# Adding the first two pairs of state products on VectorE ahead of their transposes, in a Mamba block whose order a list scheduler writes

## The chip, the cores and the metric

One NeuronCore of a Trainium2 chip runs the whole program. The metric is the device time of one execution in microseconds. The engines are named as in the profile: PE is TensorE's matmul, PEld its weight load, DVE is VectorE, ACT is ScalarE, POOL is GpSimd, and SP is the engine whose queue issues most DMAs.

## The reference

The input x has 4096 tokens of D = 1024 channels. Three residual steps follow each other, each on a layer norm of x: half an FFN with ternary weights (-1, 0, 1 times the mean absolute weight, plus a bias), a Mamba block, and the same half FFN again.

```python
x = x + 0.5 * ffn(layernorm(x))
xz = layernorm(x) @ W_in.T;  u, z = split(xz)
u = silu(conv_b + sum(conv_w[:, k] * shifted(u, k) for k in range(4)))
dt_r, B, C = split(u @ W_xproj.T)          # 64, 16 and 16 columns
dt = softplus(dt_r @ W_dt.T + b_dt)
h[n] = exp(dt * A[n]) * h_before[n] + dt * B[n] * u      # 16 states n per channel, token by token
y = sum(h[n] * C[n] for n in range(16)) + u * Dskip
x = x + (y * silu(z)) @ W_out.T
x = x + 0.5 * ffn(layernorm(x))
```

## The kernel before

The tokens are worked off in 16 chunks of T = 256 (two token tiles of 128). Inside a chunk, the Mamba block has channels on partitions and tokens along the free dimension; its 1024 channels are 8 blocks of 128, and they are worked off in two halves of 4 blocks (so a tile of a half is 128 x 4 x 256, 1024 elements in each partition).

For one half and one state n the work is this. ACT makes the decays exp(dt * A) in PSUM (line 913, two tiles of two blocks). POOL multiplies u*dt by the state's row of B (line 934) and adds what enters from the chunk before to the first token (line 941). DVE runs the recurrence over the tokens as two scans (line 966), and multiplies h by the state's row of C (line 978, in `left`): this is the product p. PE transposes p, 8 blocks of 128 x 128, into a PSUM tile y, where the transposes of all products of the half accumulate (line 998, in `summed`). So the sum over the states is taken on PE. A 17th product, n = -1, is the skip term u * Dskip, which ACT makes (line 899). When the 17 are summed, DVE multiplies y by silu(z) (line 1015, in `gate`), PE transposes the result back (line 752, in `turned`), and W_out follows (line 760), with a residual add on DVE (line 731).

Around it, per chunk: ACT and POOL make the layer norms (lines 390 to 409), PE transposes them (line 425), the FFN multiplies with x split into a high and a low part (ACT line 453, DVE line 455, PE line 497), and DVE adds its result to x (line 476). PE makes u from W_in (line 629), ACT and DVE its convolution (lines 559, 562, 574), PE the small projections for dt, B and C (lines 641, 710), and PE z from the other half of W_in (line 677), which ACT copies out and passes through silu (lines 691, 696). The rows of B and C go through DRAM and come back broadcast to all partitions (line 883).

The order of the instructions on each engine is not the order of the source. Each piece of work is a Python generator that yields requests: an engine, a duration that is written into the code, an earliest time, and a rank. `Streams.run` keeps a clock of its own, picks the request that can start first (of two with the same start, the lower rank), holds back an engine for a few hundred ns if a better rank comes soon (HOLD), and emits its instruction. It knows one resource beside the engines, `port`: requests of DVE and POOL with two operands in SBUF are not planned at the same time. Results are due at planned times kept in `ready`. Buffers are taken from and given back to pools (`Buffers`), and a request for a buffer waits until one is planned to be free. At the end the order found is fixed with dependencies, so that each engine runs its list in that order, whatever the real durations are. The pools that matter here: three PSUM banks (`banks`), three for decays, one double one for y; three tiles each for h and the products, five for the rows of B and C, five for weights. The ranks and the numbers of buffers stand at lines 52 to 61 and 208 to 226.

The z products (line 677) are issued by `rest`, which a chunk starts only when the steps behind u (`front`, from `yield DELTA` on) and both halves' dt are planned.

Of the kernel before, what the change touches and what calls it, by code (L numbers as in the profile page):

```python
# [32 lines left out]
F32 = mybir.dt.float32  # L33
F32R = mybir.dt.float32r
AF = mybir.ActivationFunctionType
ALU = mybir.AluOpType
# [16 lines left out]
REACH = 160  # L53
ISSUE, ADDED = 950, 6000
SWITCH = 1300

DECAY, ENTER, SUM, PREPARE, RECUR, GATE = 5, 1, 1, 0, 2, 2
FFN_A, NORM, U_PART, CONV, DELTA, OUT, FFN_C = 0, 0, 3, 0, 0, 2, 3

HOLD = 0, 0, 500, 100  # L60
Z = 2, 4

# [111 lines left out]
def macaron_mamba_kernel(  # L174
# [34 lines left out]
    decays = buffers(3, [P, 2, T], "da", pool_=psum)  # L209
    ys = buffers(1, [P, TT, OH], "y", pool_=psum)  # L210
    xs = buffers(6, [P, D], "x")
    xts = buffers(2, [P, NB, T], "xT")
# [3 lines left out]
    us = buffers(4, [P, HB, T], "u")  # L216
    szs = buffers(3, [P, TT, OH], "sz")
    dts = buffers(2, [P, HB, T], "dt")
# [4 lines left out]
    hs = buffers(3, [P, HB, T], "h")  # L223
    products = buffers(3, [P, HB, T], "p")
    bcs = buffers(5, [P, 2, T], "bc")
    overs = buffers(2, [P, HB, NST], "over")
# [153 lines left out]
    def stats(c, at, tiles=range(TT)):  # L380

        ln = yield from lns.take()
        sums, squares = ln[:, 0:TT], ln[:, TT : 2 * TT]
        some = slice(tiles[0], tiles[-1] + 1)
        rstd, shift, less = ln[:, 28:30][:, some], ln[:, 32:34][:, some], ln[:, 36:38][:, some]
        xn = {}
        for t in tiles:
            xn[t] = yield from tmps.take()
            end = yield act(D + 210, at[t])
            nc.scalar.activation(xn[t], x_tiles[c, t], AF.Identity, accum_out=sums[:, t : t + 1])  # L390
            end = yield pool(140, end + REACH)
            nc.gpsimd.tensor_scalar(ln[:, 36 + t : 37 + t], sums[:, t : t + 1], -1.0 / D, None, ALU.mult)
            end = yield act(D + 210, end + REACH)
            nc.scalar.activation(  # L394
                xn[t],
                x_tiles[c, t],
                AF.Square,
                bias=ln[:, 36 + t : 37 + t],
                accum_out=squares[:, t : t + 1],
            )  # L400
        end = yield pool(1050, end + REACH)
        nc.gpsimd.tensor_scalar(rstd, squares[:, some], 1.0 / D, EPS_LN, ALU.mult, ALU.add)
        nc.gpsimd.tensor_tensor(rstd, rstd, mhalf[:, some], ALU.pow)
        nc.gpsimd.tensor_tensor(shift, less, rstd, ALU.mult)
        return ln, xn, end + REACH

    def normed(c, ln, xn, t, at):
        end = yield act(D + 210, at)
        nc.scalar.activation(  # L409
            xn[t],  # L410
            x_tiles[c, t],
            AF.Identity,
            scale=ln[:, 28 + t : 29 + t],
            bias=ln[:, 32 + t : 33 + t],
        )
        return xn[t], end + REACH

# [21 lines left out]
    def ffn(c, which, rank, at, tiles=range(TT)):  # L439
# [3 lines left out]
        def split(t):  # L443
# [6 lines left out]
            def cut(g, pt, at_):  # L450
# [7 lines left out]
                if len(ends) == NB // 4:  # L458
                    ready["parts", key, t] = end + REACH
                    parts[t] = lo, hi  # L460
# [11 lines left out]
        def residual(t, cols, pf, at_):  # L472
            at_ = max(at_, (yield from when("bias", key, t)))
            end = yield dve(650, at_)
            xt = x_tiles[c, t][:, cols]
            nc.vector.scalar_tensor_tensor(xt, pf, hscl, xt, ALU.mult, ALU.add)  # L476
            if (*key, t) != ("a", 0, 1):
                banks.put(pf, end)
            ready["ffn", key, t, cols.start] = end
            if key == ("c", NC - 1):  # L480
                yield from give_out(c, t, cols, end)
# [33 lines left out]
    def as_weights_come(key, parts, residual, rank):  # L515

        for t in range(TT):
            yield from when("parts", key, t)
        y = yield from ys.take()
        groups = {(1, h): y[:, h, :] for h in range(2)}  # L520
        for h in range(2):
            groups[0, h] = yield from banks.take()
        for k in range(NB):
            yield from when("wf", k)
# [12 lines left out]
        for t in range(TT):  # L537
            los.put(parts[t][0], end)
            his.put(parts[t][1], end)
        for h in range(2):  # L540
            end = yield from when("ffn", key, 1, h * OH)
        ys.put(y, end)

# [40 lines left out]
    def front():  # L584
        for c in range(NC):
# [32 lines left out]
            for pair in range(NB // 2):  # L618
# [4 lines left out]
                for j in range(2):  # L623
# [9 lines left out]
                    weights.put(w, end)  # L633
            yield DELTA
            px = yield from banks.take()
            for half in range(2):
                at = yield from when("u", c, half)
                end = yield pe(2 * HB * T * FULL)
                for b in range(HB):
                    k = half * HB + b  # L640
                    nc.tensor.matmul(
                        px[:NXD, :T], wx[:, k, :], u[c, half][:, b, :], start=(k == 0), stop=(k == NB - 1)
                    )
            xd[c] = yield from xds.take()
            end = yield act(T, end + REACH)
            nc.scalar.copy(xd[c][RANK:NXD, 1, :], px[RANK:NXD, :T])
            for j in range(2):
                end = yield act(T)
                nc.scalar.copy(xd[c][j * RANK : (j + 1) * RANK, 0, :], px[:RANK, :T])
            banks.put(px, end)  # L650
            bc_dram[c] = dram.tile([NST, 2, T], F32, tag="bc", name=f"bcd_{c}")
            for j in range(2):
                part_ = slice(RANK + j * NST, RANK + (j + 1) * NST)
                nc.sync.dma_start(bc_dram[c][:, j, :], xd[c][part_, 1, :])
            ready["bc", c] = end + 2500
            yield from delta(c, 0, end + REACH)
            order.spawn(rest(c, xT), DELTA)

    def rest(c, xT):
        yield from delta(c, 1, 0)  # L660
        xds.put(xd[c], order.now + 2000)
        queue = streamed(z_weights, NB, 3, Z[0])
        for half in range(2):
# [72 lines left out]
    def turned(c, half, yT):  # L736
# [8 lines left out]

        yield from when("gate", c, half)
        for t in range(TT):
            pt = yield from banks.take()
            end = yield pe(HB * P * TURN)
# [24 lines left out]
    def back():  # L774
        for c in range(NC - 1):
            yield OUT
            queue = streamed(lambda i, w: out_weights(i // 2, i % 2, w), NB, 3, OUT)
            yT = []
# [20 lines left out]
            for t in range(TT):  # L799
                yield from give_out(c, t, slice(0, D), ends[t])  # L800
                xs.put(x_tiles.pop((c, t)), order.now + 6000)
        yield from last(NC - 1)
# [74 lines left out]
    def fetch():  # L877
        for c, half, n in items:
# [8 lines left out]
            coming[c, half, n] = bc  # L887
            ready["come", c, half, n] = order.now + 4000

# [13 lines left out]
    def decaying():  # L903
        for c, half, n in items:
# [3 lines left out]
            for j in range(2):  # L908
# [10 lines left out]
                decay[c, half, n, j] = da  # L919
                ready["decay", c, half, n, j] = end + REACH  # L920
            if n + 1 == NST:
# [3 lines left out]
    def enter():  # L925
        for c, half, n in items:
# [15 lines left out]
            entering[c, half, n] = h  # L942
            ready["enter", c, half, n] = end + REACH
            if n + 1 == NST:
# [9 lines left out]
    def recur():  # L954
        behind = None
        for c, half, n in items:
# [4 lines left out]
            for j in range(2):  # L961
# [6 lines left out]
                if behind and j == 0:  # L968
                    yield from left(*behind)
            order.spawn(leave(c, half, n, h, end + REACH), ENTER)  # L970
            behind = c, half, n, h
        yield from left(*behind)

    def left(c, half, n, h):
# [5 lines left out]
        product[c, half, n] = p  # L980
        ready["product", c, half, n] = end + REACH
        order.spawn(give(c, half, n, h, end), ENTER)

    def give(c, half, n, h, at):
# [3 lines left out]
    def summed():  # L988
        for c, half, n in items:
            yield from when("product", c, half, n)  # L990
            if n < 0:
                y = yield from ys.take()
            p = product.pop((c, half, n))
            end = yield pe(D * TURN)

            for t in range(TT):
                for b in range(HB):
                    nc.tensor.matmul(  # L998
                        y[:, t, b * P : (b + 1) * P],
                        p[:, b, t * P : (t + 1) * P],  # L1000
                        ident,
                        start=(n < 0 and b == 0),
                        stop=(n == NST - 1 and b == HB - 1),
                        is_transpose=True,
                        skip_group_check=True,
                    )
            products.put(p, end)
            if n + 1 == NST:
                order.spawn(gate(c, half, y, end + REACH), GATE)

    def gate(c, half, y, at):
        yield from when("z", c, half)
        z = sz[c, half]
        end = yield dve(1170, at)
        nc.vector.tensor_tensor(flat(z), flat(y), flat(z), ALU.mult)
        ys.put(y, end + REACH)
        ready["gate", c, half] = end + REACH

# [80 lines left out]
```

## Time and profile before

| what | us |
|---|---|
| median of 3 runs | 2726.5 (2725.86 to 2727.03) |
| profiled execution, whole | 2725.84 |
| its span, first to last instruction | 2724.1 |
| mean granted TensorE clock | 0.983 |
| transposes of products on PE, line 998, x4352 | 572.5 busy |
| z products on PE, line 677, x2048 records | 474.7 busy |
| scans on DVE, line 966, x1024 | 1207.7 busy, 1206 ns each |
| decays on ACT, line 913, x2048 | 938.6 busy |
| h of POOL, line 934, x512 | 1223.2 busy, 421.7 idle before them |
| table loads on ACT, 181 in all | 1283 ns each |

A row of the profile gives the line, the engine, the operation, what it writes and reads, how often; then its busy time and the mean ns of one, and behind the second bar how long the engine stood idle just before it, and for whom. Busy time of several rows of PE may overlap, since the next matmul starts before the last has drained. A matmul in f32 leaves two records.

### The profile page before, as it was taken

Reading aid. Unit: us, or ns where it says so; the run is one execution under the profiler, and the core shown is the slowest. Engines: PE = TensorE matmul, PEld = TensorE weight load, DVE = VectorE, ACT = ScalarE, POOL = GpSimd, SP = SyncE. Lnnn points to the kernel's source line nnn. Section 1 sums busy time; section 2 is a strip of 40 time slices with the busy share of each in tenths; the row PEclk is TensorE's granted clock in tenths of the full one; section 3 lists DMA queues with packets and bytes.
Section 4 is the critical chain, followed back from the end, with each engine's and each line's share of the span. In section 5 each row is a group of like instructions: output and inputs, shape, how many; then the busy total and the mean of one; then the engine's idle time right before and its main releaser. Section 6 shows DMA issues by size and latency. Waiting matters only on the chain. (4 is left out here: it accounts for less than half of the span.)

```text
span 2724.1 us, 41050 instructions
## 1 busy us (share of the span) xinstructions
PE 2568.1 (94%) x14082; PEld 2199.6 (81%) x14082; DVE 2288.3 (84%) x2404; ACT 2001.4 (73%) x4202; POOL 1815.6 (67%) x1657
## 2 busy tenths in 40 slices
PE   5797989999999999999999999999999999999988
PEld 4686878888788787888878788887888878788866
DVE  4498898978899798888879799898889879788883
ACT  3678677787877778777787877778787777877662
POOL 0367767766677585767757577686767857577761
PEclk9897999999999999999999999999999999999999
DMA  4443536455454545546554454655545554554533
GB/s 158 146 130 103 168 106 216 132 166 149 134 173 140 179 151 153 155 129 184 166 162 144 140 167 132 182 162 155 153 140 167 159 172 146 150 157 133 182 85 109
DMA packets 218553, 410.82 MB, mean 151 GB/s; under 512 B 19172, under 2 KB 85860, under 8 KB 218344
## 3 DMA queue, kind: packets, MB, share of 16 engines
q1 hardware_dynamic: 209128, 374.65, 43.3%
q0 software_dynamic: 9216, 33.56, 6.8%
q8 instruction: 110, 1.80, 0.3%
q14 instruction: 99, 0.81, 0.1%
HBM read 390.82 MB, written 17.31 MB: 150 GB/s over the span
## 5 line engine op out<-in xcount | busy, mean ns | idle before, releaser
L934 POOL TENSOR_TENSOR h<-u,bc 128x1024 f32<-128x1024 f32 x512 | 1223.2, 2389 | 421.7 <-ACT da L913 171.1
L966 DVE TENSOR_TENSOR_SCAN h<-da,h 128x512 f32<-128x512 f32 x1024 | 1207.7, 1206 | 125.6 <-ACT da L913 99.7
L913 ACT ACTIVATE da<-dt,pr 128x255 f32<-128x255 f32 x2048 | 938.6, 473 | 61.9 <-DVE h L966 32.9
L978 DVE TENSOR_TENSOR p<-h,bc 128x1024 f32<-128x1024 f32 x512 | 658.7, 1286 | 6.6 <-PE y L998 6.4
L998 PE MATMUL y<-ident,p 128*128 128x128 f32 x4352 | 572.5, 278 | 79.5 <-DVE p L978 61.1
L998 PEld LDWEIGHTS y<-ident,p 128*128 128x128 f32 x4352 | 503.9, 143 | 151.5 <-DVE p L978 95.4
L629 PE MATMUL bank<-xT,weight 128*128 128x256 f32 x2048 | 474.7, 382 | 11.4 <-ACT u L562 8.6
L677 PE MATMUL bank<-weight,xT 128*128 128x256 f32 x2048 | 474.7, 380 | 9.2 <-DMA weight<-in_w_in 9.2
L760 PE MATMUL bank<-weight,u 128*128 128x256 f32 x2016 | 467.3, 381 | 2.2 <-DMA weight<-in_w_out 1.9
L629 PEld LDWEIGHTS bank<-xT,weight 128*128 128x128 f32 x2048 | 378.6, 190 | 69.9 <-ACT u L562 21.3
L677 PEld LDWEIGHTS bank<-weight,xT 128*128 128x128 f32 x2048 | 380.2, 191 | 56.7 <-ACT da L913 9.9
L760 PEld LDWEIGHTS bank<-weight,u 128*128 128x128 f32 x2016 | 370.9, 191 | 47.2 <-DMA weight<-in_w_out 2.1
L949 ACT COPY state<-h 128x4 f32<-128x4 f32 x512 | 99.2, 194 | 292.5 <-DVE h L966 287.5
L941 POOL TENSOR_TENSOR h<-h,over 128x4 f32<-128x4 f32 x512 | 262.5, 513 | 25.2
L497 PE MATMUL bank<-wf,lo 128*128 128x512 f32 x976 | 252.3, 400 | 3.7 <-DVE lo L455 2.4
L574 DVE SCALAR_TENSOR_TENSOR u<-up,pr,u 128x256 f32<-128x256 f32 x384 | 206.4, 570 | 55.2 <-ACT u L562 42.6
L497 PE MATMUL bank<-wf,hi 128*128 128x512 f32 x976 | 245.8, 394 | 0.0
L497 PEld LDWEIGHTS bank<-wf,lo 128*128 128x128 f32 x976 | 177.7, 188 | 48.4 <-issue 4.0
L497 PEld LDWEIGHTS bank<-wf,hi 128*128 128x128 f32 x976 | 181.7, 188 | 43.0 <-issue 4.3
L865 POOL TENSOR_TENSOR over<-pr,dt 128x64 f32<-128x64 f32 x32 | 24.9, 778 | 211.3 <-ACT dt L722 211.3
L476 DVE SCALAR_TENSOR_TENSOR x<-bank,hscl,x 128x512 f32<-128x512 f32 x124 | 91.2, 737 | 71.9 <-PE bank L497 71.8
L425 PE MATMUL bank<-ident,tmp 128*128 128x128 f32 x756 | 115.9, 285 | 27.1 <-ACT tmp L409 23.4
(98 smaller groups left out, 2125.0 us busy)
## 6 DMA issues: line engine op xcount, KB each, us to landing
bc<-bcd SPq DMA_DIRECT2D x512, 256.0 KB, 3.7
weight<-in_w_out SPq DMA_DIRECT2D x128, 512.0 KB, 5.1
weight<-in_w_in SPq DMA_DIRECT2D x128, 512.0 KB, 3.7
weight<-in_w_in SPq DMA_DIRECT2D x256, 256.0 KB, 4.2
x<-hbias POOLq DMA_DIRECT2D x64, 512.0 KB, 7.9
x<-in_x SPq DMA_DIRECT2D x32, 512.0 KB, 7.3
out<-x SPq DMA_DIRECT2D x30, 512.0 KB, 4.9
weight<-in_w_ffn SPq DMA_DIRECT2D x5, 512.0 KB, 7.4
```

The costliest lines, as they stand in the source:

```text
L425: nc.tensor.matmul(pt[:, j * P : (j + 1) * P], xn[:, k * P : (k + 1) * P], ident, start=(j == 0), stop=(j == 3), is_transpose=True, skip_g ...
L497: nc.tensor.matmul(pf, x[:, k, :], wf[:, k, cols], start=(x is lo and k == 0), stop=(x is hi and k == NB - 1),)
L574: nc.vector.scalar_tensor_tensor(ub, up[:, k : k + T], tap, ub, ALU.mult, ALU.add)
L629: nc.tensor.matmul(pp[:, j, :], wt[:, k, :], xT[:, k, :], start=(k == 0), stop=(k == NB - 1))
L677: nc.tensor.matmul(pp[:, t, :], xT[:, k, t * P : (t + 1) * P], wt[:, :, i, :], start=(k == 0 and t == 0), stop=(k == NB - 1), skip_group_c ...
L760: nc.tensor.matmul(po[:, t, :], yT[:, b, t * P : (t + 1) * P], wt[:, b, :], start=(half == 0 and t == 0 and b == 0), stop=(half == 1 and b ...
L913: nc.scalar.activation(da[:, i, 1:], dt[c, half][:, b, 1:], AF.Exp, scale=a_neg[:, half * HB + b, n : n + 1],)
L934: nc.gpsimd.tensor_tensor(h, u[c, half], bc[:, 0:1, :].to_broadcast([P, HB, T]), ALU.mult)
L941: nc.gpsimd.tensor_tensor(h[:, :, 0], h[:, :, 0], over[c, half][:, :, n], ALU.add)
L966: nc.vector.tensor_tensor_scan(rows_, flat(da), rows_, 0.0, ALU.mult, ALU.add)
L978: nc.vector.tensor_tensor(p, h, bc[:, 1:2, :].to_broadcast([P, HB, T]), ALU.mult)
L998: nc.tensor.matmul(y[:, t, b * P : (b + 1) * P], p[:, b, t * P : (t + 1) * P], ident, start=(n < 0 and b == 0), stop=(n == NST - 1 and b = ...
```

## The change

Six things change together.

1. A new constant PAIRED = range(0, 4, 2) names states 0 and 2. Behind the product of such a state, the new `paired` adds the product of the state before it (the skip term before 0, state 1 before 2) on DVE, in one flat 128 x 1024 addition in place, after the next state's second scan. `summed` passes over the states -1 and 1. The product pool grows from 3 to 4 tiles.
2. y is two PSUM tiles, one for each token tile, instead of one double one. `gate` runs for each token tile, 512 columns at a time, and `turned` waits for each token tile's gate.
3. The z products leave `rest` and become a stream of their own (`gates`), started right behind u with rank Z[0] = 1, and so do the steps to dt (`steps`), whose two halves of the first projection no longer stand together.
4. Planned times: products, decays, entering states and normed tiles are taken to be ready 300 ns later than before (the four LATE constants); a bias load is taken to need 9000 instead of 6000, a row of B and C 3000 instead of 4000; x tiles are taken to be free at once after their store is issued.
5. Ranks, HOLD and the prefetch of the output weights (2 instead of 3) change.
6. Buffers: x 7 instead of 6, rows of B and C 6 instead of 5, silu(z) 2 instead of 3. The two normed tiles of a layer norm are taken together.

```diff
-ISSUE, ADDED = 950, 6000
+ISSUE, ADDED = 950, 9000
...
-DECAY, ENTER, SUM, PREPARE, RECUR, GATE = 5, 1, 1, 0, 2, 2
-FFN_A, NORM, U_PART, CONV, DELTA, OUT, FFN_C = 0, 0, 3, 0, 0, 2, 3
-HOLD = 0, 0, 500, 100
-Z = 2, 4
+LATE_P, LATE_D, LATE_E, LATE_N = 300, 300, 300, 300
+PAIRED = range(0, 4, 2)
+DECAY, ENTER, SUM, PREPARE, RECUR, GATE = 4, 2, 1, 0, 5, 4
+FFN_A, NORM, U_PART, CONV, DELTA, OUT, FFN_C = 0, 2, 3, 1, 0, 2, 3
+HOLD = 100, 0, 250, 100
+Z = 1, 4
...
-    ys = buffers(1, [P, TT, OH], "y", pool_=psum)
-    xs = buffers(6, [P, D], "x")
+    ys = buffers(TT, [P, OH], "y", pool_=psum)
+    xs = buffers(7, [P, D], "x")
...
-    szs = buffers(3, [P, TT, OH], "sz")
+    szs = buffers(2, [P, TT, OH], "sz")
...
-    products = buffers(3, [P, HB, T], "p")
-    bcs = buffers(5, [P, 2, T], "bc")
+    products = buffers(4, [P, HB, T], "p")
+    bcs = buffers(6, [P, 2, T], "bc")
...
+            order.spawn(gates(c, xT), Z[0])
+            order.spawn(steps(c), DELTA)
...
-        yield from when("gate", c, half)
         for t in range(TT):
+            yield from when("gate", c, half, t)
             pt = yield from banks.take()
...
-            queue = streamed(lambda i, w: out_weights(i // 2, i % 2, w), NB, 3, OUT)
+            queue = streamed(lambda i, w: out_weights(i // 2, i % 2, w), NB, 2, OUT)
...
                 if behind and j == 0:
                     yield from left(*behind)
+                elif behind:
+                    yield from paired(*behind[:3])
...
-        ready["product", c, half, n] = end + REACH
+        if n not in PAIRED:
+            ready["product", c, half, n] = end + REACH + LATE_P
...
+    def paired(c, half, n):
+        if n not in PAIRED:
+            return
+        yield from when("product", c, half, n - 1)
+        q = product.pop((c, half, n - 1))
+        p = product[c, half, n]
+        end = yield dve(1132, 0, True)
+        nc.vector.tensor_tensor(flat(p), flat(p), flat(q), ALU.add)
+        products.put(q, end)
+        ready["product", c, half, n] = end + REACH + LATE_P
...
     def summed():
         for c, half, n in items:
+            if n + 1 in PAIRED:
+                continue
...
-            end = yield pe(D * TURN)
             for t in range(TT):
+                if first:
+                    y[t] = yield from ys.take()
+                end = yield pe(OH * TURN)
...
-    def gate(c, half, y, at):
+    def gate(c, half, t, y, at):
         yield from when("z", c, half)
-        z = sz[c, half]
-        end = yield dve(1170, at)
-        nc.vector.tensor_tensor(flat(z), flat(y), flat(z), ALU.mult)
+        z = sz[c, half][:, t, :]
+        end = yield dve(650, at)
+        nc.vector.tensor_tensor(z, y, z, ALU.mult)
```

## The prediction

> **What bounds the kernel now.** I read the page's busy shares and slices first, then a table of 85-us windows, then TensorE's waits in the steady middle, and last single stretches of the timeline. The chain that ended last covers only the final 60 us, so it cannot say what sets the other 2660.
>
> ```profile
> PE 2568.1 (94%) x14082; PEld 2199.6 (81%) x14082; DVE 2288.3 (84%) x2404; ACT 2001.4 (73%) x4202; POOL 1815.6 (67%) x1657
> ...
> PE   5797989999999999999999999999999999999988
> ...
> PEclk9897999999999999999999999999999999999999
> ```
>
> TensorE (PE) is busy 94% of the span. Its gaps lie in the first 425 us, where the granted clock falls too, and in the last 100. The windows (columns after the length: busy us of PE, PEld, DVE, ACT, POOL) show the middle:
>
> ```profile
> 425.00:510.00 85.00, 83.18 (x480) 71.99 (x479) 79.58 (x76) 61.06 (x133) 64.87 (x53) 1.00 0.57 175
> ...
> 935.00:1020.00 85.00, 83.64 (x474) 73.54 (x473) 79.43 (x85) 61.87 (x141) 64.73 (x57) 1.00 0.51 157
> 1020.00:1105.00 85.00, 81.95 (x448) 68.82 (x447) 68.75 (x74) 68.66 (x135) 52.61 (x50) 1.00 0.58 164
> ```
>
> PE is at 96 to 98% in both kinds of window. VectorE (DVE) swings between 79.5 us (94%), where mostly states are worked off, and 69 us (81%), where the FFN and the convolution lie. Over long stretches:
>
> ```profile
> 100.00:2665.00 2565.00, 2451.38 (x13579) 2104.46 (x13578) 2230.64 (x2315) 1953.01 (x4119) 1802.64 (x1613) 0.99 0.51 153
> 425.00:2550.00 2125.00, 2066.68 (x11507) 1775.75 (x11506) 1844.03 (x1934) 1635.36 (x3432) 1484.14 (x1344) 1.00 0.52 156
> ```
>
> In the middle PE idles 2125 - 2067 = 58 us, DVE 281 us. PE sets the pace, DVE is second at 87%. What PE's 58 us wait for:
>
> ```profile
> PE y L998 <- DVE p L978: 22.7, 34, 1.3
> PE y L998 <- DVE sz L1015: 15.8, 12, 1.3
> PE bank L752 <- DVE x L476: 10.1, 12, 0.8
> ```
>
> No wait is over 1.3 us. Only the two ends have real holes: 35.00 - 18.13 = 17 us idle in 209:244 and 55.00 - 37.69 = 17 us in 2610:2665, both behind products of DVE.
>
> **Removed: 64 transposed products.** Each half of a chunk transposes 17 products (skip term and 16 states), 8 instructions each. With states 0 and 2 in PAIRED, -1 is added to 0 and 1 to 2, so 15 are left: 32 halves x 2 = 64 products, 512 of the 4352 transposes. What one is worth on PE's path is seen where PE never stops:
>
> ```profile
> 2541.84 1.04 PE L998 MATMUL y<-ident,p 128*128 128x128 f32 x8
> 2542.71 1.89 PE L760 MATMUL bank<-weight,u 128*128 128x256 f32 x8
> 2544.44 1.04 PE L998 MATMUL y<-ident,p 128*128 128x128 f32 x8
> ```
>
> The row lasts 1.04 us, but the next begins 0.87 us after its start, since the ends overlap. The Trainium skill (Trainium Kernel Development and Optimization, "Performance Expectations") calls matmul busy time a bad metric because matmuls are pipelined, and trusts the busy share of weight loads. That speaks against this change: by weight loads PE would be at 81% and not bound. By the matmul group's busy time (572.5 us / 4352) the 512 are worth 67 us, by its weight loads (503.9 / 4352) 59 us, by start to start 64 x 0.87 = 56 us. I take the last, and hold against the rule's 81% that the middle shows 2.7% of PE time without a matmul and no wait over 1.3 us. About 6 of the 64 (second half of chunk 0, the last chunk) lie where PE waits for DVE anyway. The gain is 58 x 0.87 = -50.6 us (ends: -45, -59).
>
> **Added: 64 adds on DVE.** The rows nearest to a flat 128x1024 add of two SBUF operands:
>
> ```profile
> L978 DVE TENSOR_TENSOR p<-h,bc 128x1024 f32<-128x1024 f32 x512 | 658.7, 1286 | 6.6 <-PE y L998 6.4
> ...
> L455 DVE TENSOR_TENSOR lo<-bank,hi 128x512 fp32r<-128x512 f32 x125 | 83.0, 677 | 52.3 <-ACT hi L453 52.1
> ...
> L860 DVE TENSOR_TENSOR u<-u,dt 128x1024 f32<-128x1024 f32 x32 | 39.1, 1220 | 38.7 <-ACT dt L722 31.6 <-ACT p L899 7.0
> L1015 DVE TENSOR_TENSOR sz<-y,sz 128x1024 f32<-128x1024 f32 x32 | 39.0, 1218 | 13.6 <-ACT sz L696 7.8 <-PE y L998 5.1
> ```
>
> L860 has that very shape: 64 x 1.22 = 78 us of DVE. The gate in two parts adds 2 x 0.68 (L455, half the size, one PSUM operand) - 1.22 = 0.14 us, times 32 is 4 us. In all +82 us of DVE. In the middle PE now needs 2125 - 25 halves x 2 x 0.87 = 2081 us, and DVE has 1844 + 25 x 2.58 = 1908 us of work in it: 92%. DVE's idle time must fall from 281 to 173. Much of it is PE's own pace: L476 waits 64.5 us for PE, L731 26.9, L455 47.8 for a copy behind PE, 139 in all. These go when DVE falls behind. The 62.7 us before scans that wait for ScalarE's decays need not. And windows at 92 to 94% DVE already stand beside PE at 98%. So I charge the middle nothing, with ends of -11 (half of the 22.7 goes, since products are now planned 300 ns later) and +45.
>
> Each add has queued behind it the next state's scan and product, and PE's next transposes wait for those. Where PE waits for DVE, at the two ends, an add is on the path: about 3 x 1.2 = +3.6 us (0, +7).
>
> **The shared port.** A flat add also shuts POOL out:
>
> ```profile
> 1242.07 1.41 DVE L978 TENSOR_TENSOR p<-h,bc 128x1024 f32<-128x1024 f32 x1
> 1242.47 1.07 POOL L941 TENSOR_TENSOR h<-h,over 128x4 f32<-128x4 f32 x1
> ...
> 1243.61 2.36 POOL L934 TENSOR_TENSOR h<-u,bc 128x1024 f32<-128x1024 f32 x1
> ```
>
> L941 takes 0.21 us alone (1250.75 in the same timeline) and here 1.07, ending with the product; the 2.36-us L934 begins only then. The skill says so too (SBUF — State Buffer, "SBUF: two separate sides": a DVE operation with two SBUF inputs and a reading GpSimd operation hold one port pair exclusively, for the whole instruction). By the rows of DVE alone an add costs 1.22 us of one engine; by the rule it costs POOL 1.22 us too. Estimated occupancy of the pair: 512 x (2.36 + 0.21) + 512 x 1.20 + 39 (L860) + 384 x 0.47 (L574) = 2150 us of the 2565 (84%); with 78 more, 2228 of about 2520 (88%). POOL's L934 idles 421.7 us before it starts, which covers 78. I charge 0 (0 to +30, inside the +45 above).
>
> **Moved.** The gate per token tile: PE's 17.4 us behind L1015 go, since the next half's first transpose now comes after an add. In the new instruction order, though, the second half's L752 stands directly behind that half's last transposes, and on DVE one scan (1.21) and the first gate (0.68) lie between product and gate: PE is through after 0.97 us, the gate after 1.9, so some 1.2 us x 16 = 19 us of new wait, partly in place of the old 10.1 us for banks. I take -1 (-17, +20). The z products as a stream: same matmuls, earlier. PE's one 9.2-us wait for their weights near 100 us may go, but PE then only stands longer at 209:244, where it waits for the recurrence; 0. Their DMAs and the output weights (two ahead, not three) stand in SP's queue with the state loads, which wait 1199.6 us in 395 waits (3.0 us each) for product buffers; two ahead are 2 x 3.46 us of products on PE against 5.1 us to land, so covered; without cover up to +15. Twelve more table loads in the new ACT order (193 against 181) x 1.28 us = 15 us of ACT, which has 27% free: 0. POOL's queue keeps its 64 bias loads (7.9 us to land; planned with 9 us instead of 6, so DVE's L476 stands later in its queue): 0. The new order ends with 8 and then 2 products in a row with nothing between (before 4 and 2); each such wait is about 2.4 us today, part of the backlog is done by then: +4 (0, +12).
>
> **Sum.** 2725.8 (profiled execution: span 2724.1 + 1.7 around it) - 50.6 + 3.6 - 1 + 4 = 2681.8; the median of the runs is 0.7 higher: 2682 us.
>
> **Rivals.** (1) PE keeps the pace, as summed: 2682, with ends of 2642 (waits for products and gates go too) and 2710. Chance 0.62. (2) DVE binds for part of the way. Between 100 and 2665 us it will have 2231 + 82 = 2313 us of work. The case above needs it at 92% of the stretch; at 91% the stretch is 2542 us instead of 2565, and the time 2726 - 23 = 2703; at 90.5%, 2717. For: DVE's long average is 87% today. Against: the windows at 92 to 94%. Chance 0.18, taken at 2708. (3) Slower: DVE's idle time does not shrink. Its queue is in order, and an add before a scan pushes everything behind it: the h buffers come free later, so POOL's next L934 starts later, and port and decays come out of step. Then the 82 us come on top and the removed transposes only leave PE waiting: up to 2808. It decides where fewer than 82 of the 334 us of DVE idle in that stretch go, that is at DVE below 90%. With half of that regained it is 2767. Chance 0.2. (4) The change does not do what it says, because new waits in a row of transposes eat the 50 us: 2726. This is the border of (2) and (3) and its chance, 0.07, is a part of theirs.
>
> **The numbers.** Predicted 2682. About 0.2% (5 us) is what a measurement can tell from no change. Case (1) and 0.13 of (2) are faster: 0.75. The other 0.05 of (2) and 0.02 of (3), with (4), are the same: 0.07. The rest of (3) is slower: 0.18. The range of 8 in 10 leaves some 7% below 2642, which only the best ends of the waits reach, and 12% above 2755, the far part of (3). The likeliest case alone is 2642 to 2710.
>
> **What would show it.** Right: the transposes fall to 3840, the add's group reads x64 at 1.2 to 1.3 us, PE's share stays at 94% or above, and DVE's rises to about 88% of the span, with less wait before L476 and L455. The wait of transposes for L1015 is gone; a wait of L752 for the gate of about 1 us, 16 times, stands in its place. Wrong: PE's share falls below 92% and its waits for products or sums pass 100 us, with DVE above 90% in most windows (2); or DVE's idle before scans, behind POOL's h or ACT's da, grows (3).

## The result, and the profile after

The changed kernel takes 2696.6 us (median of 4 runs, 2694.3 to 2698.1) against 2726.2 us of the kernel before (4 runs): a ratio of 0.989, with a 95% interval of 0.9878 to 0.9903. That is 30 us less, where 44 less were forecast. The profiled execution took 2698.1 us.

The same rows of the page as before: busy shares, then TensorE's slices and its granted clock.

```profile
PE 2522.3 (94%) x13570; PEld 2150.7 (80%) x13570; DVE 2436.7 (90%) x2500; ACT 2012.7 (75%) x4214; POOL 1802.3 (67%) x1657
...
PE   5988899999999999999999999999999999999887
...
PEclk8998899999999999999999999999999999999888
```

PE does 45.8 us less (2568.1 to 2522.3) and DVE 148.4 us more (2288.3 to 2436.7), where 82 were expected. PE's idle time rises from 156.0 to 174.0 us. The last slices are thinner than before, in PE and in clock. The transposes of products, before and after:

```profile
L998 PE MATMUL y<-ident,p 128*128 128x128 f32 x4352 | 572.5, 278 | 79.5 <-DVE p L978 61.1 <-DVE sz L1015 17.4
L1022 PE MATMUL y<-ident,p 128*128 128x128 f32 x3840 | 513.5, 279 | 72.9 <-DVE p L984 65.0 <-DVE p L999 6.0
```

Two windows of the changed kernel (columns as before: length, then busy us of PE, PEld, DVE, ACT, POOL, granted clock):

```profile
425.00:2400.00 1975.00, 1916.53 (x10504) 1639.75 (x10503) 1866.45 (x1902) 1548.33 (x3253) 1394.98 (x1270) 1.00 0.51 158
100.00:2637.00 2537.00, 2408.68 (x13078) 2058.41 (x13078) 2370.41 (x2402) 1953.14 (x4111) 1778.29 (x1602) 0.98 0.50 155
```

and the kernel before in the same middle:

```profile
425.00:2400.00 1975.00, 1921.08 (x10699) 1650.93 (x10698) 1713.47 (x1797) 1522.11 (x3193) 1381.00 (x1254) 1.00 0.53 157
```

PE stays at 97%. DVE goes from 87 to 94.5% of the middle: its mean is now about the highest share that it reached in 85-us windows before (79.58 of 85, 93.6%). Its costliest groups show where the work and the idle time went:

```profile
L984 DVE TENSOR_TENSOR p<-h,bc 128x1024 f32<-128x1024 f32 x512 | 684.8, 1338 | 0.1
...
L999 DVE TENSOR_TENSOR p<-p,p 128x1024 f32<-128x1024 f32 x64 | 127.7, 1995 | 0.0
L479 DVE SCALAR_TENSOR_TENSOR x<-bank,hscl,x 128x512 f32<-128x512 f32 x124 | 91.1, 735 | 35.6 <-PE bank L499 33.3 <-PE bank L530 2.2
L458 DVE TENSOR_TENSOR lo<-bank,hi 128x512 fp32r<-128x512 f32 x125 | 82.7, 673 | 22.9 <-ACT hi L456 22.8
```

L999 is the added add: 1995 ns, not the 1220 of the row it was priced by. The products are longer too, 1338 ns instead of 1286, which is 26 us; 16 of these are there without the adds as well (e3: 674.6 us for the same row, against 658.7 before). The idle time before the FFN's adds and subtractions (L479, L458, before: L476, L455) has halved, as forecast: 71.9 to 35.6 and 52.3 to 22.9.

What an add waits for is seen in the timeline of the middle (all engines, a part of 1341 to 1346 us):

```profile
1341.11 1.21 DVE L969 TENSOR_TENSOR_SCAN h<-da,h 128x512 f32<-128x512 f32 x1
...
1341.31 2.40 POOL L937 TENSOR_TENSOR h<-u,bc 128x1024 f32<-128x1024 f32 x1 [1.32 <-ACT xd L650]
...
1342.24 2.56 DVE L999 TENSOR_TENSOR p<-p,p 128x1024 f32<-128x1024 f32 x1
...
1343.80 1.07 POOL L944 TENSOR_TENSOR h<-h,over 128x4 f32<-128x4 f32 x1
```

POOL's h starts during the scan that stands between product and add, and runs to 1343.71. The add's record begins at 1342.24, but ends 1.09 us after POOL's end, which is about the length of an add: it stood still until POOL was through. Of the 64 adds, 18 last 1.21 us, one a little more, 14 about 1.85 and 31 about 2.5. It works the other way as well: POOL's L944, 4 elements wide, lasts 1.07 us and ends with the add.

PE's waits in the middle (425 to 2550 us), in order of their sum:

```profile
PE bank L628 <- ACT u L561: 26.4, 39, 0.9
PE y L1022 <- DVE p L984: 22.4, 27, 7.0
PE bank L628 <- ACT up L558: 9.8, 13, 0.8
PE bank L755 <- ACT da L916: 9.3, 13, 0.7
```

The wait of transposes for the gate (15.8 us before) is gone, and no wait of L755 for a gate has come in its place. The u products L628 now wait 36 us for ACT to clear PSUM banks (2.4 us before, then L629). In the last 270 us the transposes wait more than before (then 15.8 us for products and 2.9 for a gate, 2454 to 2725 us); the changed kernel from 2426 us to its end:

```profile
PE y L1022 <- DVE p L984: 26.8, 12, 7.0
PE y L1022 <- DVE p L999: 5.6, 1, 5.6
```

### The profile page after: what moved, and what is told of

It reads as the page before. It is cut to its first block, busy times and chain, and to the rows that moved or that the text cites. A ratio compares the mean times of both kernels' runs of the same rounds, so it can differ in the third digit from the quotient of the medians.

```text
span 2696.3 us, 40026 instructions
## 1 busy us (share of the span) xinstructions
PE 2522.3 (94%) x13570; PEld 2150.7 (80%) x13570; DVE 2436.7 (90%) x2500; ACT 2012.7 (75%) x4214; POOL 1802.3 (67%) x1657
## 4 chain that ended last, share of the span: by engine, by line
PE 35%; DVE 27%; ACT 15%; issue 12%; POOL 2%; DMA 2%; DVEq 0%; SPq 0%; POOLq 0%; ACTq 0%
DVE h L969 14%; PE bank L628 11%; DVE p L984 9%; PE bank L499 7%; PE bank L680 6%; ACT da L916 4%; PE y L1022 4%; PE bank L645 2%; PE bank L763 2%; DVE p L999 2%; PE bank L428 2%; ACT u L561 1%; DVE x L734 1%; POOL h L937 1%; ACT L916 1%
## 5 line engine op out<-in xcount | busy, mean ns | idle before, releaser
L937 POOL TENSOR_TENSOR h<-u,bc 128x1024 f32<-128x1024 f32 x512 | 1226.2, 2395 | 517.7 <-ACT da L916 212.0
L984 DVE TENSOR_TENSOR p<-h,bc 128x1024 f32<-128x1024 f32 x512 | 684.8, 1338 | 0.1
L1022 PE MATMUL y<-ident,p 128*128 128x128 f32 x3840 | 513.5, 279 | 72.9 <-DVE p L984 65.0
L1022 PEld LDWEIGHTS y<-ident,p 128*128 128x128 f32 x3840 | 450.1, 144 | 139.7 <-DVE p L984 92.1
L628 PE MATMUL bank<-xT,weight 128*128 128x256 f32 x2048 | 472.8, 384 | 43.7 <-ACT u L561 32.2
L628 PEld LDWEIGHTS bank<-xT,weight 128*128 128x128 f32 x2048 | 380.5, 191 | 114.9 <-ACT u L561 53.4
L944 POOL TENSOR_TENSOR h<-h,over 128x4 f32<-128x4 f32 x512 | 285.4, 557 | 27.6 <-issue 0.3
L573 DVE SCALAR_TENSOR_TENSOR u<-up,pr,u 128x256 f32<-128x256 f32 x384 | 214.5, 591 | 95.4 <-ACT u L561 92.4
L548 POOL COPY halo<-up 128x3 f32<-128x3 f32 x128 | 45.7, 357 | 165.1 <-ACT up L558 164.9
L428 PE MATMUL bank<-ident,tmp 128*128 128x128 f32 x756 | 116.0, 285 | 32.0 <-ACT tmp L412 21.9
L558 ACT COPY up<-bank 128x256 f32<-128x256 f32 x128 | 47.0, 367 | 121.5 <-PE bank L628 119.1
```

The source lines that it names most:

```text
L428: nc.tensor.matmul(pt[:, j * P : (j + 1) * P], xn[:, k * P : (k + 1) * P], ident, start=(j == 0), stop=(j == 3), is_transpose=True, skip_g ...
L573: nc.vector.scalar_tensor_tensor(ub, up[:, k : k + T], tap, ub, ALU.mult, ALU.add)
L628: nc.tensor.matmul(pp[:, j, :], wt[:, k, :], xT[:, k, :], start=(k == 0), stop=(k == NB - 1))
L937: nc.gpsimd.tensor_tensor(h, u[c, half], bc[:, 0:1, :].to_broadcast([P, HB, T]), ALU.mult)
L944: nc.gpsimd.tensor_tensor(h[:, :, 0], h[:, :, 0], over[c, half][:, :, n], ALU.add)
L984: nc.vector.tensor_tensor(p, h, bc[:, 1:2, :].to_broadcast([P, HB, T]), ALU.mult)
```

## The experiments

Times are medians with their ratio to the kernel before on the same chip. "PE idle" and "DVE idle" are the span less the engine's busy time.

| kernel | us | ratio, 95% interval | PE idle | DVE idle |
|---|---|---|---|---|
| before | 2726.2 | 1 | 156 | 436 |
| changed | 2696.6 | 0.989 (0.9878 to 0.9903) | 174 | 260 |
| no pairs (e1) | 2730.8 | 1.0018 (1.0009 to 1.0026) | 163 | 395 |
| pairs alone (e2) | 2880.7 | 1.0566 (1.0552 to 1.0581) | 286 | 441 |
| adds left out (e3) | 2678.4 | 0.9826 (0.9813 to 0.9839) | 163 | 366 |
| convolution's rank (e4) | 2696.5 | 0.9891 (0.9878 to 0.9905) | 177 | 259 |
| one pair (e5) | 2754.1 | 1.0100 (1.0083 to 1.0117) | 199 | 362 |
| four pairs (e6) | 2903.4 | 1.0657 (1.0632 to 1.0682) | 355 | 340 |
| add at the product, planned anew (e7) | 2817.5 | 1.0337 (1.0322 to 1.0353) | 272 | 396 |
| z after dt (e8) | 2887.5 | 1.0593 (1.0578 to 1.0609) | 321 | 449 |
| transposes back (e10) | 2734.0 | 1.0030 (1.0019 to 1.0042) | 165 | 293 |
| add at the product, same order (e11) | 2702.1 | 0.9916 (0.9902 to 0.9929) | 181 | 280 |
| add twice (e12) | 2760.8 | 1.0128 (1.0115 to 1.0142) | 222 | 256 |
| add planned at 2000 (e13) | 2813.8 | 1.0326 (1.0312 to 1.0340) | 266 | 387 |

Two theories stood at first. A: the 15 us that are missing to the forecast went to the adds, whose time on DVE and at the port was priced too low. B: they went to the new order of everything else, whose sign is the new wait before L628. C came after e2: the order that the planner writes weighs more than the work in it.

Two kinds of edit must be kept apart. Some touch what the planner sees (PAIRED, ranks, planned times), so that a new order is written. Others (e3, e10, e11, e12) only change what is emitted at a place of the order found, so the rest keeps its place.

**e1: the change without the pairs.**

```diff
-PAIRED = range(0, 4, 2)
+PAIRED = range(0)
```

> The changed kernel with PAIRED empty: 17 transposed products again, no adds; ranks, streams, buffers and gates of the change stay. Theory A (the gain of the removed transposes is paid back on DVE by adds that take 2.0 us instead of 1.22): the transposes come back on PE (+56 us), and the 128 us of adds leave DVE, so 2720 to 2735 us, DVE near 2300 us busy. Rival B (the new ranks and planned times lose 34 us, in PE's new waits for ACT's convolution copies before L628; pairing by itself works as summed): those waits stay, 2745 to 2760 us.

Measured 2730.8, inside A's range and outside B's. Streams, gate per token tile, ranks and planned times without the pairs cost 4.5 us. That total says nothing of their parts: the waits before L628 are in it (17.9 us for L561 in 425 to 2400), and so is a wait for the gate of 8.3 us. But 4.5 us in all are too few for B.

**e2: the pairs alone, in the kernel before.** The new `paired`, its calls and the fourth product tile; all else as before.

```diff
+PAIRED = range(0, 4, 2)
-    products = buffers(3, [P, HB, T], "p")
+    products = buffers(4, [P, HB, T], "p")
```

> The kernel before with nothing but the pairs: states -1 and 1 added to 0 and 2 on DVE, 15 transposed products, a fourth product tile. Theory A: the adds meet POOL's h here too and DVE pays part of the gain back, 2690 to 2705 us. Rival B: without the new ranks the full gain shows, 2665 to 2680 us, with L629's waits for ACT as small as before (8.6 us).

Measured 2880.7: both theories miss, by far. DVE has nearly the same work as in the changed kernel (2437.3 us busy), but does not get nearer to its bound: it idles 441 us. PE's longest wait in 425 to 2400 us is a new one:

```profile
PE bank L679 <- DMA weight<-in_w_in: 68.6, 16, 7.4
```

z's products (L679) wait for their weights. So the pairs, planned with the old ranks and streams, are a loss of 154 us, and the gain of the whole is no sum of the gains of its parts. The order is a new one here too, so the run does not say what the adds alone do to the old order.

**e3: the changed kernel, its adds not issued.** The order is kept; the skip term and state 1 are missing from y.

```diff
-        nc.vector.tensor_tensor(flat(p), flat(p), flat(q), ALU.add)
```

> The changed kernel with the same planned order on every engine, but the 64 adds themselves are not issued (so the skip term and state 1 are missing from y). It measures what the adds cost in place. Theory A: 128 us of DVE time vanish, PE no longer runs dry behind products, 2660 to 2675 us. Rival B: PE's waits before L628 set the time and stay, 2688 us or more. If the adds were free beside PE, as the prediction charged the middle: 2690 to 2697.

Measured 2678.4. The 64 adds cost 18.2 us where they stand, neither nothing nor all. The middle without them:

```profile
425.00:2400.00 1975.00, 1923.29 (x10581) 1650.18 (x10580) 1775.99 (x1868) 1552.62 (x3278) 1374.38 (x1280) 1.00 0.52 160
```

DVE falls to 89.9% of it. Over the whole span its busy time falls by 126.4 us, yet the span of the profile is only 20 us shorter: the other 106 us come back as idle time of DVE (366 instead of 260). On PE the 20 us are 11 us less idle time, 9 of them in the middle, and 9 us less busy time for the same instructions, at a mean clock of 0.980 instead of 0.977.

**e4: another rank for the convolution.**

```diff
-FFN_A, NORM, U_PART, CONV, DELTA, OUT, FFN_C = 0, 2, 3, 1, 0, 2, 3
+FFN_A, NORM, U_PART, CONV, DELTA, OUT, FFN_C = 0, 2, 3, 0, 0, 2, 3
```

> The changed kernel with CONV = 0 as before, nothing else: the convolution's copies on ACT come ahead of others again. Theory A: PE's waits before L628 (43.7 us) fall, but PE only waits elsewhere for DVE, 2690 to 2702 us. Rival B: 2660 to 2675 us.

Measured 2696.5. The edit changes no place of any instruction on any engine, so this is the changed kernel once more: it tells nothing of the ranks, but shows that the time and the idle times come again within 0.1 and 3 us.

**e5 and e6: one pair, and four.**

```diff
-PAIRED = range(0, 4, 2)
+PAIRED = range(0, 2, 2)
```

```diff
-PAIRED = range(0, 4, 2)
+PAIRED = range(0, 8, 2)
```

> The changed kernel with PAIRED = range(0, 2, 2): only the skip term is added to state 0, 16 transposed products in each half. Theory A (each removed transposed product is worth 0.83 us of time, 52 us for 64, each add in place costs 0.28 us, 18 for 64): half of both, 2731 - 26 + 9 = 2714 us. Theory C (the time is that of the order which the planner happens to find, and moves by tens of us with any edit): anything outside 2704 to 2724 us.

> The changed kernel with PAIRED = range(0, 8, 2): four pairs, 13 transposed products in each half, 128 adds. If the exchange stays linear (theory A without a limit on DVE): 2731 - 104 + 36 = 2663 us. If DVE becomes the bound, since its busy time rises from 2437 to some 2565 us: at the 93.4% that it reaches between 100 and 2637 us now, 2565 / 0.934 less what lies outside, so 2690 to 2740 us, and PE's waits for products and sums over 100 us.

Measured 2754.1 and 2903.4. Half the pairs do not give half the gain: the kernel is slower than with none. With four, the adds last 2069 ns, but DVE is busy for only 88% of the span, and PE waits 85.5 us for products and 51.1 for normed tiles in 425 to 2400 us. In that stretch DVE is busy 91% and PE 90%, both less than in the changed kernel. So neither engine's work alone sets this time. That the order written for it does is what is left, but no run with four pairs kept an order fixed.

**e7: the add right behind its product, planned anew.** In the old place the next state's second scan lies between.

```diff
                 if behind and j == 0:
                     yield from left(*behind)
-                elif behind:
                     yield from paired(*behind[:3])
```

> The changed kernel with each add on DVE right behind the product that it takes, ahead of the next scan instead of behind it. Now 46 of 64 adds stand 0.6 to 1.4 us behind a running h of POOL, which starts while the scan between product and add leaves the port free. If that scan is what lets POOL in, the adds fall to 1.2 us, DVE to 2390 us busy, and the time to 2685 to 2692. If a waiting POOL instruction takes the port between product and add, the adds rise to 2.5 us or more and the time stays or rises, 2697 to 2715.

Measured 2817.5. Now 36 of the 64 adds take 1.21 to 1.23 us, the mean is 1779 ns, and PE idles 272 us, of which 64.5 in 425 to 2400 us are before L428, for the normed tiles of ACT (L412). Since place and order change together, the place alone is left to e11.

**e8: z's products back behind dt.** All else as changed.

```diff
-            order.spawn(gates(c, xT), Z[0])
-            order.spawn(steps(c), DELTA)
+            order.spawn(steps(c, xT), DELTA)
...
+        order.spawn(gates(c, xT), Z[0])
```

> The changed kernel with the z products started only when both halves' dt are planned, as in the kernel before; pairs, ranks, planned times, buffers and the gate per token tile stay. If the early stream of z products is what lets the pairs pay (pairs alone gave 2881 us, with 93.8 us of PE waiting for z's weights): 2750 us or more, with those waits back. If ranks and planned times do it: 2690 to 2710.

Measured 2887.5, 191 us over the changed kernel. With z late, this plan does not pay. But e5, e6, e7 and e13 leave z early, are planned anew as well, and lose 57 to 207 us, so it is not shown that the start of z is the cause. The weights of z, which the expectation named, are not what PE waits for here (7.0 us over the span); in 425 to 2400 us it is:

```profile
PE bank L428 <- ACT tmp L412: 75.7, 16, 11.0
PE y L1022 <- DVE p L984: 57.2, 36, 3.6
```

PE stands up to 11 us before the next layer norm's transposes. That it has no z products left to fill in when products and norms are late fits this, but was not tried on its own. The same wait for ACT's norms stands in e6 and e7 (51.1 and 64.5 us), not in e2 and e13 (0.9 and 5.2 us): the bad orders do not share one wait.

**e10: the same order, each pair's sum transposed twice.** y counts the paired states twice.

```diff
+                for b in range(HB if n in PAIRED else 0):
+                    nc.tensor.matmul(y[t][...], p[...], ident, start=False, stop=False, ...)
```

> The changed kernel with the order of every engine kept, but each of the 64 summed pairs is transposed twice in a row, so 17 transposed products in each half as before (y then counts those pairs twice). It measures on PE what the removed 512 transposes were worth in this order. Theory A: start to start 64 x 0.87 = 56 us, so 2740 to 2753 us. If PE has slack, since DVE at 93% of its stretch bounds in part: under 2730.

Measured 2734.0. The 512 transposes are worth 37.3 us in the changed kernel, between the two expectations: 0.58 us for each product of 8, where 0.87 had been read off a stretch in which PE never stopped. In the two profiles they add 53 us to PE that no other row covers; 9 of these come out of PE's idle time, and its other rows are 8 us shorter, at a granted clock of 0.980 instead of 0.977. Why the clock is higher was not tried.

**e11: the same order, the add issued directly behind its product.** Nothing else moves.

```diff
         # in left, behind the product
+        if n in PAIRED:
+            nc.vector.tensor_tensor(flat(p), flat(p), flat(product[c, half, n - 1]), ALU.add)
         # in paired
-        nc.vector.tensor_tensor(flat(p), flat(p), flat(q), ALU.add)
```

> The changed kernel in the same order but for one thing: each add is issued on DVE right behind its product, ahead of the scan, without planning anew. The run that planned anew (2817 us) mixed this with another order. If the scan between lets POOL's h into the port: adds fall from 2.0 to about 1.2 to 1.5 us, 2685 to 2693. If a waiting POOL takes the port between product and add, 2697 to 2710. A time near 2817 would say that the place of the add itself did that harm; theory C says it did not.

Measured 2702.1, 5.5 us over the changed kernel. The adds are shorter, and DVE is busy 18 us less, but the time is not:

```profile
L986 DVE TENSOR_TENSOR p<-p,p 128x1024 f32<-128x1024 f32 x64 | 107.4, 1678 | 2.2
```

POOL's h goes from 2395 to 2465 ns, 36 us in all: 47 of the 512 now last over 3.0 us, where 7 did, most of them because they come 0.10 us after an add has begun, as here:

```profile
113.58 1.23 DVE L986 TENSOR_TENSOR p<-p,p 128x1024 f32<-128x1024 f32 x1
...
113.68 3.41 POOL L937 TENSOR_TENSOR h<-u,bc 128x1024 f32<-128x1024 f32 x1 [2.18 <-issue]
```

So the place of the add moves the wait from DVE to POOL and gains nothing; and e7's loss of 121 us comes from its new order and not from the place.

**e12: the same order, each add issued twice.** The second term of a pair counts twice.

```diff
         nc.vector.tensor_tensor(flat(p), flat(p), flat(q), ALU.add)
+        nc.vector.tensor_tensor(flat(p), flat(p), flat(q), ALU.add)
```

> The changed kernel in the same order with each add issued twice in a row (the pair's second term counts twice). With none it is 2678, with one 2697. If one more 64 x 1.2 us of DVE is paid like the first, 18 us for 128 us of DVE time: 2707 to 2715. If DVE is the bound by now: the whole 78 us, 2750 to 2775.

Measured 2760.8. The two groups of adds:

```profile
L999 DVE TENSOR_TENSOR p<-p,p 128x1024 f32<-128x1024 f32 x64 | 128.1, 2001 | 0.0
...
L1000 DVE TENSOR_TENSOR p<-p,p 128x1024 f32<-128x1024 f32 x64 | 79.1, 1235 | 2.2
```

The second adds take 79.1 us and cost 64.2 us of time. DVE's busy time rises by 66.0 us in all, since the products are 12 us shorter. The middle:

```profile
425.00:2400.00 1975.00, 1882.71 (x10229) 1595.35 (x10230) 1865.67 (x1907) 1515.79 (x3176) 1362.49 (x1243) 1.00 0.51 155
```

DVE is at the same 94.5% as in the changed kernel (1865.67 beside 1866.45 of 1975 us), and PE has fallen from 97 to 95.3%. DVE's idle time over the span went from 366 us without adds to 260 with them and to 256 with two each. The first adds are paid out of idle time, the second are not: there is none left to pay with in this order.

**e13: the changed kernel, planned with the add's measured time.**

```diff
-        end = yield dve(1132, 0, True)
+        end = yield dve(2000, 0, True)
```

> The changed kernel, planned anew with the adds' measured 2000 ns in place of 1132; no other edit, and the same instructions in number. If knowing the true cost mends the order: 2680 to 2695. If the planned order alone moves the time by tens of us, whatever the edit means (theory C): outside 2680 to 2710, with PE idle in 425:2400 well above the 58 us of the changed kernel, most of it before the transposes of normed tiles (L428) and of products.

Measured 2813.8. A truer figure makes a worse order. PE idles 136 us in 425 to 2400, and 112.1 of these before transposes, for products. There is one hole of about 7.5 us in 13 of the 16 chunks, as here on PE:

```profile
1288.10 1.97 PE L1022 MATMUL y<-ident,p 128*128 128x128 f32 x8 [7.53 <-DVE p L984]
```

PE has run through the products that were ready, and the one it waits for waits itself: DVE stands 3.25 us before the scan at 1284.71, behind POOL's L944, at the change from one half to the next. The adds are shorter in this order (1645 ns). No version tried beats the changed kernel with all of its work in it.

## Why the prediction was right, and where a term was off

The exchange works as described: 512 transposes less on PE, 64 adds more on DVE, and a gain. The time of 2697 lies 15 us over the forecast. Step by step:

**Transposes, -50.6 us.** Their row falls by 59.0 us (572.5 to 513.5), and PE as a whole by 45.8. The difference is overlap: records of neighbouring matmuls lie over each other, and what the transposes add to PE by themselves falls by 48.9 us (441.2 to 392.3, PE's busy time less that of all its other records), near the forecast. So 0.87 us per product is about right as a share of PE. But in place they are worth only 37.3 us of time (e10): some 9 us of them fall into time in which PE would have stood idle, and against 8 more PE's other rows were shorter.

**Adds, +3.6 us, the middle and the port at nothing.** This is the term that failed, in size, and in the middle. Measured in place it is 18.2 us (e3), inside the ends given. The sign that the forecast named for itself, adds at 1.2 to 1.3 us, did not show. Two parts of the working were wrong. The price of 1.22 us came from a row whose operations do not meet POOL (all 32 of L860 last 1.19 to 1.23 us). The row quoted beside it, of a 1.07-us L941 under a product, spoke of POOL being shut out by DVE and was priced at 0; the rule of the Trainium skill weighed there (SBUF — State Buffer, "SBUF: two separate sides") says that whichever operation starts first holds the pair through its whole length. That binds both sides, and here much of it fell on DVE: 46 of the 64 adds waited, and the mean is 1995 ns. By the row alone the 64 adds are 78 us, as measured they are 128. The products' 26 us are most of the rest; 10 of them go when the adds go (e3), the other 16 come with the new order. So DVE had 2370 us of work in 100 to 2637, not 2313. Its share, 93.4%, was above the 92% that the forecast needed, and PE still held 97% of the middle. But with 57 us more work of DVE than forecast, it did not come free. Rival (2), DVE binding for part of the way, is what e3 and e12 show: adds cost 18 of 126 us, and the next ones 64 of 79.

The two terms must not be read as parts of one sum. Taking away the adds gives back 18 us, putting back the transposes costs 37, and neither is its engine's whole time, since another engine stands close behind. Both at once in the same order was not run.

**Gates and banks, -1 us.** The wait for the gate went as said. The 19 us that I put in its place, L752 (now L755) waiting for its own gate, did not come: waits of PE for a gate are 2.4 us over the whole span, none of them in the middle. What came was a wait that I had not named, L628 for banks, 34 us more. PE's idle time in the middle rose only by 5 us (55.2 in 425 to 2454, 60.4 in 425 to 2426). e1 puts all of this together at +4.5 us, within the ends.

**The end, +4 us.** The transposes' waits in the last 270 us, for products and before also for a gate, rose from 18.7 to 32.4 us. That is 13.7, just over the end of 12 that was given. In e3, without adds, they are 27.7, in e1, without pairs, 11.3: most of it comes with the order that the pairs get at the end, where products stand in a row, and 4.7 us with the adds themselves, which were priced at 3.6 for both ends. All of PE's idle time there is 41 us with the adds and without (28 before). The holes cost clock as well: in the last 270 us PE was granted 0.98 and 0.90 before, 0.91 and 0.84 now (185 and 85 us), and this had no place in the sum.

By PE's own account the span's 27.8 us are: -48.9 for what the transposes add by themselves, +3.2 for all other rows together, which do the same work at a mean clock of 0.977 instead of 0.983, and +18.0 of idle time. The last 270 us alone have 13 us more idle time.

**Rival (3), slower because DVE's idle time does not shrink,** is not this kernel, but its outcome is what its neighbours show: in e2, e7, e8 and e13 DVE idles 387 to 449 us with the same adds, and they are slower than the kernel before by 88 to 161 us. The forecast's limit, DVE below 90% from 100 us to 59 us before the end, parts them from the changed kernel: they are at 87 to 89%, it is at 93.4%. That they are slow in the way described there, by h buffers that come free late, is not shown; their waits differ.

On this point the forecast had luck. It read the gates and the ends off the new order, but charged the middle nothing because the old order had windows with both engines full. That this order would stay full all the way had no term, and in e13 the same instructions in another order take 117 us more.

Open stays which rule of the planner leads to the bad orders, and what the ranks alone are worth, which e4 did not test.

## What to carry to other kernels

Before work is moved to a second engine, price it by rows that share its port with the same neighbours, not by the quietest row of its shape, and look at how much idle time the receiving engine can still give: here the first 126 us cost 18, the next 79 cost 64. Where an order is planned, test a part by changing what is emitted at a fixed place of the order; edits that the planner sees moved this kernel by up to 191 us (e8) with the same instructions. A forecast for such a kernel should be made from the two orders themselves, holes at the ends included, since a hole costs both its length and the clock after it.

## What the hardware showed that was not expected

Two DVE operations back to back do not keep the port against POOL. In e11, with the add directly behind the product, 51 adds took 1.22 to 1.26 us, but 13 took 3.42 or 3.43, about one h of POOL (2.4 us) more than an add. One of the 13:

```profile
614.46 1.20 DVE L984 TENSOR_TENSOR p<-h,bc 128x1024 f32<-128x1024 f32 x1
614.80 0.91 POOL L407 TENSOR_TENSOR ln<-ln 128x2 f32<-128x2 f32 x1
...
615.68 2.35 POOL L937 TENSOR_TENSOR h<-u,bc 128x1024 f32<-128x1024 f32 x1
615.69 3.42 DVE L986 TENSOR_TENSOR p<-p,p 128x1024 f32<-128x1024 f32 x1
```

In all 13 a small operation of POOL (L407, two elements wide) stands waiting under the product and is through about 0.05 us after it; the h behind it on POOL follows at once and begins about 0.01 us ahead of the add. In 34 others h comes 0.10 us after the add has begun, and then h waits. The second adds of e12, with a mean of 1235 ns, met small waiting operations too (L944 or L395 in 48 of 64 cases), but no h directly behind one. So what costs is a long operation queued behind the one that gets in at the seam.

A wait of PE costs more than its length, if it is long enough. At the end of the changed kernel (transposes of one product each, the idle time before them in brackets):

```profile
2574.06 1.04 PE L1022 MATMUL y<-ident,p 128*128 128x128 f32 x8
2576.34 1.09 PE L1022 MATMUL y<-ident,p 128*128 128x128 f32 x8 [1.24 <-DVE p L984]
2579.70 1.97 PE L1022 MATMUL y<-ident,p 128*128 128x128 f32 x8 [2.27 <-DVE p L984]
```

The last took nearly twice as long as the others. The granted clock (third figure from the right) around it:

```profile
2525.00:2578.00 53.00, 51.20 (x288) 45.41 (x286) 51.58 (x50) 30.50 (x75) 41.44 (x29) 1.00 0.43 133
2579.00:2585.00 6.00, 5.30 (x25) 4.98 (x25) 4.41 (x6) 5.21 (x10) 3.75 (x4) 0.50 0.45 89
```

From 292 to 2500 us, where PE never waits over 0.93 us, it is 1.00; in the kernel before it is 1.00 from 412 to 2619, with waits of up to 1.56 us. In the profiles of the two kernels, the transposes of every product behind a hole of over 3 us took 1.97 us, those behind holes of 0.5 to 1.5 us took 1.09 to 1.10, and behind holes between these some took the one and some the other.

Kernels with holes on PE also ran their matmuls at a lower clock in the middle: e8 was granted 0.96 in 425 to 2614 us and its PE was busy 41 us longer than the changed kernel's with the same instructions (2563.4 beside 2522.3). Of these, 34 us are in the two groups that stand behind its holes, L428 (138.7 beside 116.0) and L1022 (525.2 beside 513.5).
